# Two cross-attention layers on one core: the first layer's output projection with three of its products split once more, and the second layer's queries spread over earlier work

## The chip, the cores and the metric

The kernel runs on one core of a Trainium2 chip. The metric is the time of one execution in microseconds (us). TensorE (PE in the profile) multiplies, VectorE (DVE) adds, ScalarE (ACT) evaluates functions and copies, GpSimd (POOL) does some elementwise work and issues some transfers, SyncE (SP) issues the others. All data are 32-bit floats.

## The reference, cut to what matters

Two cross-attention layers follow each other; B=8 batches of 100 rows with 1024 features attend to 1444 context rows with 512 features.

```python
# layer 0
Q = query @ Wq + bq;  K = ctx @ Wk + bk;  V = ctx @ Wv + bv
weights = softmax(Q @ K.T / 32)            # over the 1444 context rows
x = query + (weights @ V) @ Wo + bo
# layer 1: Q and K likewise from x and ctx, but the softmax runs over the 100 rows
w = softmax((x @ Wq + bq) @ (ctx @ Wk + bk).T / 32, axis=rows)
y = w @ (ctx @ Wv + bv) + x
out = (y - mean) * rsqrt(var + 1e-6) * gamma + beta
```

## The kernel before

**Weights first.** The kernel multiplies weights with each other, so that keys and values are never formed. For layer 0 it makes `wqk0` = Wq Wk^T (1024 x 512) and `wvo` = Wv Wo (512 x 1024), for layer 1 `wqk1`. "Queries" are then x times wqk, 512 features long, and are multiplied with the context itself. The attended context (512 long, `A0T`) is projected with `wvo` onto the residual `xT`.

**Seven products instead of eight.** Large products are cut into 2x2 blocks and computed with seven block products and sums of blocks (the Strassen-Winograd scheme). `seven_products` (L202) does this for the projections. S and T are the sums of left and right blocks; the banks X, Y, Z, W are accumulators in PSUM. Some block products are cut once more in the same way by `inner_product` (L255), a generator with seven steps, each one smaller product into one bank and its addition to the result. It keeps its second and fourth sums in the place of its operands, and makes them after its first and second product.

**PSUM.** There are eight accumulator banks: six in the pool that `bank` (L68) takes from, two in that of `bank2` (L71). `bank2` serves the weighted rows (`weighted_rows`, L831) and the products named z and w.

**Layer 0 per batch.** `alternated(b)` (L1130) runs 48 steps; each is one small matmul of the weighted context rows of batch b (tile A, line L837) and one piece of the scores of batch b+2 (tile s, line L866). For batches 6 and 7 there are no scores left.

**The projection** (`project0`, L956) has two halves, j=0 and j=1, for features 0 to 511 and 512 to 1023 of `xT`. Each is a `seven_products` with 400-wide right operands; a block product is four matmuls of 128x128 by 128x400. The first two products of half j=0 are issued between batches 6 and 7, the other twelve after batch 7. All their results are added to `xT` on VectorE. The sums of weight blocks are made during batch 1 (`value_sums`).

**The second layer's queries** (`queries(1, ...)`, L616) come next. The steps are X = A11 B11; then Y = S1 T1; an inner product z; X with S2 T2; X with S3 T3 alternating with an inner product w; and, after the scores of batch 0 of layer 1, Y with S4 B22. Their block products are eight matmuls of 128x128 by 128x400, their inner steps two of 128x128 by 128x200. The banks of X and Y hold over nearly all of this. The sums S1, S2 lie in tiles of the tag `row`, S3 and S4 in the place of `wqk1`. `key_bias_sums` (L590) adds eight scaled copies of `xT` on VectorE (tile `kb`), and `key_biases` (L603) reduces them to one number per row and batch (tile `c`); both stand after the first five query steps, and the scores of batch 0 come after them.

**What sets the order.** TensorE executes in program order (`manual_schedule`). On the other engines a planner orders the instructions, by the order of the program and by when it takes operands to be ready; an instruction wrapped in `keep_in_program_order` is pinned behind the instruction that stands before it on its engine. The object `vector` does this to every VectorE instruction issued while `vector.in_order` is true. In `project0` nothing is pinned; in the second queries most is.

**Buffers.** `unit` (L74) gives one of ten rotating 6 KB-per-partition buffers. The context tiles cT and c are loaded into them through SP's queue, each load waiting for its buffer to come free; scratch and constants of later stages use the same ten. The tag `AT` (two buffers) holds the attended context, later T1 and T2 of the queries; the tag `gT` (three) holds the queries and the projection's sums.

Of the kernel before, what the change touches and what calls it, by code (L numbers as in the profile page):

```python
# [25 lines left out]
F32 = mybir.dt.float32  # L26
AF = mybir.ActivationFunctionType
ALU = mybir.AluOpType
# [3 lines left out]
P = 128  # L32
# [23 lines left out]
def two_layer_cross_attention(ctx: ExitStack, tc: tile.TileContext, a: dict, out: bass.AP):  # L56
# [11 lines left out]
    def bank(name):  # L68
        return psum.tile([P, 512], F32, tag="ps", name=name)

    def bank2(name):  # L71
        return psum2.tile([P, 512], F32, tag="ps2", name=name)

    def unit(name):  # L74
        return stream.tile([P, E + L], F32, tag="unit", name=name)

    def wide(name):
        return work.tile([P, LC, GT], F32, tag="AT", name=name, bufs=2)

    def row(name):  # L80
        return work.tile([P, E], F32, tag="row", name=name, bufs=3)
# [98 lines left out]
    def combine(to, x, y, op, engine=vector):  # L180
        for t, p, q in zip(to, x, y):
            engine.tensor_tensor(t, p, q, op)
# [69 lines left out]
        add(0, 1, Y)  # L252
        yield

    def inner_product(name, lhs, rhs, nb, width, t, put, add, right=None):  # L255

        h, w = nb // 2, width // 2

        def quarters(x, n):
            if len(x) == 1:
                return ([x[0][:, 2 * k : 2 * k + 2, c]] for c in halves(n) for k in range(2))
            return ([x[2 * k + i][:, c] for i in range(2)] for c in halves(n) for k in range(2))

        def room(x, t):
            t = t.rearrange("p (i n) -> p i n", i=2)
            return [t] if len(x) == 1 else [t[:, i, :] for i in range(2)]  # L270

        A11, A12, A21, A22 = quarters(lhs, nb * P)
        B11, B21, B12, B22 = quarters(rhs, width)
        S1, T1 = room(lhs, t[:, : 2 * h * P]), room(rhs, t[:, 2 * h * P : 2 * h * P + 2 * w])

        T2, T3, T4 = B11, B12, B21
        if right:
            T1, T2, T3, T4 = right
        combine(S1, A21, A22, ALU.add)
        combine(T1, B12, B11, ALU.subtract)  # L280
        combine(A21, A11, A21, ALU.subtract)
        combine(T3, B22, B12, ALU.subtract)

        def product(ps, left, right, fresh):
            half_product([ps], left, right, fresh, h, w)

        def steps():
            X = bank(f"{name}_x")
            product(X, A11, B11, True)
            put(0, 0, X)  # L290
            combine(T2, B22, T1, ALU.subtract)
            combine(A11, S1, A11, ALU.subtract)
            yield
            Z = bank2(f"{name}_z")
            product(Z, A12, B21, True)
            add(0, 0, Z)
            combine(T4, B21, T2, ALU.subtract)
            combine(A12, A12, A11, ALU.subtract)
            yield
            Y = bank(f"{name}_y")  # L300
            product(Y, S1, T1, True)
            put(1, 1, Y)
            yield
            product(X, A11, T2, False)
            put(0, 1, X)
            yield
            W = bank2(f"{name}_w")
            product(W, A22, T4, True)
            put(1, 0, W)
            yield  # L310
            product(Y, A12, B22, False)
            add(0, 1, Y)
            yield
            product(X, A21, T3, False)
            add(1, 1, X)
            add(1, 0, X)
            yield

        return steps()

    def halves(n):
        return slice(0, n // 2), slice(n // 2, n)
# [267 lines left out]
    def key_bias_sums(name, wqbk):  # L590

        acc = work.tile([P, B * T + P - T], F32, tag="kb", name=name, bufs=1)
        nc.gpsimd.memset(acc[:, B * T :], 0.0)
        for k in range(EC):
            if k == 0:
                nc.vector.tensor_scalar(acc[:, : B * T], xT[:, k, :], wqbk[:, k : k + 1], None, ALU.mult)
            else:
                nc.vector.scalar_tensor_tensor(
                    acc[:, : B * T], xT[:, k, :], wqbk[:, k : k + 1], acc[:, : B * T], ALU.mult, ALU.add
                )  # L600
        return acc

    def key_biases(name, kb, bqbk):  # L603

# [11 lines left out]
    def queries(layer, w, u, between=None):  # L616
# [4 lines left out]
        H, nb, h = EC // 2, 2, GT // 2  # L621
        A11, A12, A21, A22 = ([w[:, k * H : (k + 1) * H, j * 256 : j * 256 + 256]] for j in range(2) for k in range(2))
        B11, B21, B12, B22 = ([xT[:, k * H : (k + 1) * H, g * GT : g * GT + GT]] for g in range(2) for k in range(2))
        S1, S2 = ([row(f"g{layer}_s{n}").rearrange("p (c l) -> p c l", c=H)] for n in (1, 2))
        T1, T2 = ([wide(f"g{layer}_t{n}")] for n in (1, 2))
        T3 = [work.tile([P, LC, GT], F32, tag="gT", name=f"g{layer}_t3", bufs=3)]
        dst = [work.tile([P, LC, GT], F32, tag="gT", name=f"g{layer}T_{g}", bufs=3) for g in range(2)]

        def put(r, g, banks):
            for j in range(2):  # L630
# [20 lines left out]
            return put, add  # L651

        def pair(n):
            return [bank(f"g{layer}_{n}{j}") for j in range(2)]

        def product(banks, lhs, rhs, fresh):
            half_product(banks, lhs, rhs, fresh, nb, GT)

        t = unit(f"g{layer}_t")

        def inner(n, lhs, rhs, put, add, right=None, at=0):
            return inner_product(f"g{layer}_{n}", lhs, rhs, nb, GT, t[:, at:], put, add, right)

        def four(t):

            return [[t[:, n, :].rearrange("p (i t) -> p i t", i=2)] for n in range(4)]

        def steps():
            X = pair("x")
            product(X, A11, B11, True)  # L670
            put(0, 0, X)
            yield
            S3, S4 = A21, A12
            if layer == 0:
                Z = pair("z")
                product(Z, A12, B21, True)
            vector.in_order = layer == 0
            combine(S1, A21, A22, ALU.add)
            vector.in_order = True
            combine(T1, B12, B11, ALU.subtract)  # L680
            combine(S2, S1, A11, ALU.subtract)
            if layer == 0:
                combine(T2, B22, T1, ALU.subtract)
                vector.in_order = False
                yield
                vector.in_order = True
                add(0, 0, Z)
            combine(S3, A11, A21, ALU.subtract)
            if layer == 0:
                combine(T3, B22, B12, ALU.subtract)  # L690
            Y = pair("y")
            product(Y, S1, T1, True)
# [22 lines left out]
            V = half_steps(X, S3, T3, False, nb, GT)  # L715
            for n, _ in enumerate(inner("w", A22, T1, *parts(1, 0))):
                next(V)
                if layer == 0 and n == 1:
                    between()
                elif layer == 0 and n == 3:  # L720

                    add(0, 1, Y)
                    _, more = parts(0, 1)
                    Q = inner("q", S4, B22, more, more, four(T2[0]), 768)
# [62 lines left out]
    run(steps)  # L787
    wqbk0 = totals("wqbk0", sums_c, 2 * EC)
    nc.vector.tensor_tensor(out_bias, out_bias, wqbk0[:, EC:], ALU.add)
    kb0 = key_bias_sums("kb0", wqbk0[:, :EC])  # L790
    wqk1, (acc_c, acc_u) = next(qk1)
    c0 = next(got[0])
    for t in prob:
# [161 lines left out]

    def project0(AS, A0):  # L956

        Bs = [[A0[g][:, 2 * k + i, :] for i in range(2)] for g in range(2) for k in range(2)]
        t12, t4 = (work.tile([P, LC, GT], F32, tag="gT", name=f"o0_t{n}", bufs=3) for n in (12, 4))
        T_ = ([t12[:, i, :] for i in range(2)], [t12[:, 2 + i, :] for i in range(2)], Bs[2], chunks(t4, 2))  # L960
        for j, (A, S) in enumerate(AS):

            def add(r, g, banks, j=j):
                e = 4 * j + 2 * r
                add_to_queries([e, e + 1], g * GT, GT, banks)

            right = None if j else (lambda n: right_sums(Bs, T_, (n,)))
            yield seven_products(f"o0_{j}", A, Bs, S, T_, 2, GT, add, add, right=right)


    def softmax1(s, parts):
# [174 lines left out]
    first_transposed(batches[0], 0)  # L1146
    run(steps)
    for b in range(B):
        if b == B - 1:

            o0 = list(project0(AS, A0))
            next(o0[0])
            next(o0[0])
        run(alternated(b, 0, softmax0, A0[b // G][:, :, b % G * T : (b % G + 1) * T]))
        for e in range(2 * b, 2 * b + 2) if 2 * b < EC else ():
            add_out_bias(e)
        if b == 0:
            sums = quarter_sums("k1")
            block_sums("u1", acc_u, sums[:, :LC, :], late=True)
            block_sums("wqbk1", acc_c, sums[:, LC : LC + EC, :], late=True)  # L1160
        if b == 1:
            got = totals("k1", sums[:, : LC + EC, :], LC + EC)
            u1, wqbk1 = got[:, :LC], got[:, LC:]
            vector.in_order = True
            AS = value_sums(wvo)
            vector.in_order = False
    next(o0[1])
    for steps in o0:
        run(steps)

    gT[1], steps = queries(1, wqk1, u1)
    run(islice(steps, 5))
    kb1 = key_bias_sums("kb1", wqbk1)
    *_, key_bias[1] = key_biases("c1", kb1, bqbk1)
    vectors = [unit(f"vectors_{j}") for j in range(2)]
    gamma, beta = (t[:, :E] for t in vectors)
    bv1 = [t[:, E:] for t in vectors]
# [5 lines left out]
    nc.gpsimd.dma_start(out=wv1, in_=a["L1_xattn_Wv"].rearrange("(c p) e -> p c e", p=P))  # L1183


    run(first_scores(0, 1, softmax1))
    run(steps)
    run(first_scores(1, 1, softmax1))

# [44 lines left out]
```

## Time and profile before

| | |
|---|---|
| median of three runs | 635.28 us (633.83 to 636.32) |
| the profiled execution | 635.93 us, of which the span from first to last instruction is 634.0 us |
| granted TensorE clock | 0.997 of full speed |
| TensorE busy | 623.5 us of the span (98%) |
| VectorE busy | 480.7 us (76%) |
| ScalarE, GpSimd busy | 157.3 us (25%), 93.5 us (15%) |
| weighted rows of batch 6, two products, weighted rows of batch 7 | 321.9 to 349.6 us |
| the other twelve products of the projection | 349.6 to 381.8 us |
| second queries up to the first scores of layer 1 | 381.8 to 413.4 us |

A line of the timeline gives start, duration, engine, source line, operation, tiles (written<-read) with the shape, and how many instructions were merged; idle time before it and what ended that stand in brackets. One 32-bit matmul shows as two records. The ends of matmuls are modelled and overlap the next start by 0.16 to 0.17 us, so durations of TensorE are taken from start to start. L163 and L96 are lines of helpers, which is why the tile's name counts there. "PEld" is the load of the stationary operand, which overlaps.

### The profile page before, as it was taken

Reading aid. Unit: us, or ns where it says so; the run is one execution under the profiler, and the core shown is the slowest. Engines: PE = TensorE matmul, PEld = TensorE weight load, DVE = VectorE, ACT = ScalarE, POOL = GpSimd, SP = SyncE. Lnnn points to the kernel's source line nnn. Section 1 sums busy time; section 2 is a strip of 40 time slices with the busy share of each in tenths; the row PEclk is TensorE's granted clock in tenths of the full one; section 3 lists DMA queues with packets and bytes.
Section 4 is the critical chain, followed back from the end, with each engine's and each line's share of the span. In section 5 each row is a group of like instructions: output and inputs, shape, how many; then the busy total and the mean of one; then the engine's idle time right before and its main releaser. Section 6 shows DMA issues by size and latency. Waiting matters only on the chain.

```text
span 634.0 us, 10421 instructions
## 1 busy us (share of the span) xinstructions
PE 623.5 (98%) x4112; PEld 531.0 (84%) x4112; DVE 480.7 (76%) x948; ACT 157.3 (25%) x369; POOL 93.5 (15%) x123
## 2 busy tenths in 40 slices
PE   9999999999999999999999999999999999999994
PEld 8886466688985999999998556756999999999992
DVE  2987979998875797666753799549777659898886
ACT  1322010206204234423230001113433240325301
POOL 2110100002110000000000001008211220544054
PEclk9999999999999999999999999999999999999998
DMA  8969946015789899999965206155899890599002
GB/s 265 297 141 317 345 132 219 1 47 113 149 288 384 279 306 305 329 300 309 318 208 184 86 0 232 48 194 192 290 298 309 317 315 17 198 330 332 28 20 85
DMA packets 51077, 135.17 MB, mean 213 GB/s; under 512 B 4242, under 2 KB 8594, under 8 KB 51030
## 3 DMA queue, kind: packets, MB, share of 16 engines
q1 hardware_dynamic: 46792, 120.85, 55.7%
q0 software_dynamic: 3840, 13.20, 8.8%
q8 instruction: 32, 0.52, 0.3%
q10 hardware_dynamic: 398, 0.47, 0.2%
q14 instruction: 15, 0.12, 0.1%
HBM read 123.36 MB, written 3.28 MB: 200 GB/s over the span
## 4 chain that ended last, share of the span: by engine, by line
PE 94%; DVE 3%; issue 1%; POOL 1%; ACT 0%; POOLq 0%; DVEq 0%
PE s L866 25%; PE A L837 25%; PE qk_x L163 7%; PE o_x L163 5%; PE g_x L163 4%; PE vo_x L163 3%; PE o_y L163 3%; PE qk_z L163 2%; PE qk_y L163 2%; PE g_y L163 2%; PE o_w L163 2%; PE o_z L163 2%; PE qk_w L163 1%; PE vo_y L163 1%; PE vo_z L163 1%; PE z L1065 1%
## 5 line engine op out<-in xcount | busy, mean ns | idle before, releaser
L837 PE MATMUL A<-w,c 120*128 120x100 f32 (+1 forms) x1536 | 247.7, 265 | 0.0
L837 PEld LDWEIGHTS A<-w,c 120*128 120x128 f32 (+1 forms) x1536 | 215.9, 190 | 0.8
L96 DVE STREAM_TRANSPOSE w<-prob 32x384 f32<-32x384 f32 (+1 forms) x256 | 143.7, 561 | 35.1 <-ACT prob L878 15.7
L866 PE MATMUL s<-cT,g1T 128*100 128x131 f32 (+2 forms) x592 | 122.9, 296 | 0.3 <-DVE g1T L96 0.3
L866 PE MATMUL s<-cT,g0T 128*100 128x131 f32 (+2 forms) x592 | 122.7, 296 | 0.0
L866 PEld LDWEIGHTS s<-cT,g1T 128*100 128x100 f32 x592 | 78.3, 167 | 9.3 <-DVE g1T L96 1.2
L866 PEld LDWEIGHTS s<-cT,g0T 128*100 128x100 f32 x592 | 78.2, 167 | 8.4 <-PE c L566 0.4
L878 ACT ACTIVATE prob<-s,c 100x393 f32<-100x393 f32 (+2 forms) x64 | 35.1, 560 | 112.7 <-PE s L866 112.4
L988 ACT ACTIVATE w<-w,negmax 120x100 f32<-120x100 f32 (+1 forms) x96 | 34.8, 364 | 82.4 <-DVE negmax L96 82.4
L898 DVE TENSOR_REDUCE maxima<-prob 100x1 f32<-100x394 f32 (+3 forms) x32 | 16.5, 528 | 24.3 <-ACT prob L878 24.0
L163 PE MATMUL qk_x<-qk 128*128 128x256 f32 x128 | 30.5, 388 | 0.0
L1183 POOL DMA_DIRECT2D wv<-in_L_xattn_Wv x1 | 0.8, 772 | 200.1 <-PE o_x L163 200.1
L1007 POOL TENSOR_TENSOR part<-w 120x500 f32<-120x500 f32 x8 | 10.9, 1363 | 113.0 <-DVE rstd L1082 28.6
L163 PEld LDWEIGHTS qk_x<-qk 128*128 128x128 f32 x128 | 24.0, 196 | 3.2 <-ACT qk L413 0.2
L632 ACT ACTIVATE g1T<-g_x,k 128x400 f32<-128x400 f32 x4 | 2.4, 594 | 69.2 <-PE g_x L163 69.0
L533 POOL DMA_DIRECT2D qk_L_xattn_bk<-qk_L_xattn_bk x5 | 4.4, 937 | 102.6 <-ACT qk_L_xattn_bk L530 92.0
L96 DVE TENSOR_TENSOR xT<-xT,o_x 128x400 f32<-128x400 f32 (+1 forms) x32 | 15.8, 539 | 4.5 <-PE o_x L163 4.3
L988 ACT ACTIVATION_READ_ACCUMULATOR w<-w,negmax 120x1 f32 (+1 forms) x96 | 17.9, 187 | 0.0
L1087 POOL TENSOR_TENSOR z<-z,vectors 100x1024 f32<-100x1024 f32 x7 | 16.5, 2357 | 8.2 <-ACT z L1086 8.2
L1065 PE MATMUL z<-ident,xT 128*100 128x128 f32 x64 | 16.3, 273 | 0.0
L96 DVE TENSOR_TENSOR w<-w,rtotal 120x400 f32<-120x400 f32 (+1 forms) x24 | 15.6, 648 | 0.7
L1086 ACT ACTIVATE z<-z,rstd 100x1024 f32<-100x1024 f32 x7 | 8.1, 1150 | 31.9 <-POOL rstd L1083 31.9
(340 smaller groups left out, 961.5 us busy)
## 6 DMA issues: line engine op xcount, KB each, us to landing
cT<-in_ctxT SPq DMA_DIRECT2D x64, 722.0 KB, 6.5
c<-in_ctx SPq DMA_DIRECT2D x48, 768.0 KB, 7.9
c<-in_ctx SPq DMA_DIRECT2D x16, 512.0 KB, 7.3
vo<-in_L_xattn_Wo SPq DMA_DIRECT2D x8, 512.0 KB, 9.8
qk<-in_L_xattn_WqT SPq DMA_DIRECT2D x8, 512.0 KB
qk<-in_L_xattn_WqT SPq DMA_DIRECT2D x15, 256.0 KB, 6.2
c<-in_ctx SPq DMA_DIRECT2D x16, 224.0 KB, 6.2
xT<-in_xT SPq DMA_DIRECT2D x2, 1600.0 KB
```

The source lines that it names most:

```text
L96: ins = getattr(nc.vector, op)(*args, **kw)
L163: nc.tensor.matmul(banks[n // per][:, n % per * width : (n % per + 1) * width], lhs[i][:, n * P : (n + 1) * P], rhs[i], start=(fresh and i ...
L533: nc.gpsimd.dma_start(out=to, in_=t, accum_op=ALU.add)
L837: nc.tensor.matmul(ps[:, k * T : (k + 1) * T], c[m // CQ][:r, m % CQ, k * P : (k + 1) * P], w[:r, m, :], start=(m == 0 and k == 0), stop=( ...
L866: nc.tensor.matmul(banks[n // per][:T, cuts[n] - o : cuts[n + 1] - o], q[:, k, t0 : t0 + T], cT[k][:, cuts[n] : cuts[n + 1]], start=(k == ...
L878: nc.scalar.activation(p[:, part], ps[:T, : part.stop - part.start], AF.Identity, bias=key_bias[layer][:T, b : b + 1], scale=SCALE,)
L898: nc.vector.tensor_reduce(maxima[:, n : n + 1], p[:, part], AX.X, ALU.max)
L988: nc.scalar.activation(w[:r, m0 + m, :], w[:r, m0 + m, :], AF.Exp, bias=negmax[:r, m : m + 1], accum_out=total[:r, m : m + 1])
L1007: add(part, w[:MR, 0:5, :], w[:MR, 5:10, :], ALU.add)
L1065: nc.tensor.transpose(ps[:T, e * P : (e + 1) * P], xT[:, 4 * j + e, b * T : (b + 1) * T], ident)
L1086: nc.scalar.activation(z, z, AF.Copy, scale=rstd)
L1087: nc.gpsimd.tensor_tensor(z, z, beta[:T], ALU.add)
```

## The change

- `inner_product` works for operands of two pieces as well as four, and can make all its eight sums ahead of its products, into scratch (`ahead`). `spare` says which pool its banks z and w come from.
- `project0` is written out: both halves run interleaved in one order. Three products of half j=1 (z, w and q) are split by `inner_product`; the others stay. The first two products of half j=0 are issued one matmul at a time among the 48 steps of batch 6, and the seven steps of the split z among those of batch 7. From batch 7 on, VectorE's instructions are pinned.
- `queries(1)`: the sums S1, S2, S3 are issued during batch 7, T1 in the middle of the projection. S1 and S2 lie in `unit` buffers. The banks of Y come from the pool of two, those of the inner products all from the pool of six. In layer 0's queries the sum S1 is no longer pinned.
- The eight additions of `kb` for layer 1 are issued one by one from query step n=3 on; their reduction follows, pinned; its last part (one matmul and three small VectorE instructions) stands before the last two matmuls of the first scores.

```diff
-    def inner_product(name, lhs, rhs, nb, width, t, put, add, right=None):
+    def inner_product(name, lhs, rhs, nb, width, t, put, add, right=None, ahead=False, spare=bank2):
...
         combine(S1, A21, A22, ALU.add)
         combine(T1, B12, B11, ALU.subtract)
-        combine(A21, A11, A21, ALU.subtract)
+        combine(S3, A11, A21, ALU.subtract)
         combine(T3, B22, B12, ALU.subtract)
+        if ahead:
+            second()
+            fourth()
...
-            Z = bank2(f"{name}_z")
+            Z = spare(f"{name}_z")
             product(Z, A12, B21, True)
             add(0, 0, Z)
-            combine(T4, B21, T2, ALU.subtract)
-            combine(A12, A12, A11, ALU.subtract)
+            if not ahead:
+                fourth()
...
         def pair(n):
-            return [bank(f"g{layer}_{n}{j}") for j in range(2)]
+
+            return [(bank2 if layer and n == "y" else bank)(f"g{layer}_{n}{j}") for j in range(2)]
...
+            spare = bank if layer else bank2
+            return inner_product(f"g{layer}_{n}", lhs, rhs, nb, GT, t[:, at:], put, add, right, spare=spare)
...
+            if layer:
+                combine(S1, A21, A22, ALU.add)
+                yield
+                combine(S2, S1, A11, ALU.subtract)
+                yield
+                combine(S3, A11, A21, ALU.subtract)
+                yield
+            T1, T2 = ([wide(f"g{layer}_t{n}")] for n in (1, 2))
+            if layer:
+                combine(T1, B12, B11, ALU.subtract)
+                yield
...
             for n, _ in enumerate(inner("w", A22, T1, *parts(1, 0))):
                 next(V)
+                if layer:
+                    yield
...
+        yield first()
+        vector.in_order = True
+        yield inner("z", 1, 0, 0, A_[1], B21, room[:, :512], right)
+        combine(T1, B12, B11, ALU.subtract)
+        X_ = pair("x")
+        product(X_, A_[0], B11, True)
+        combine(T2, B22, T1, ALU.subtract)
+        add(1, 0, 0, X_)
+        Y = pair("y")
+        product(Y, S[0], T1, True)
+        combine(T4, B21, T2, ALU.subtract)
+        combine(T3, B22, T3, ALU.subtract)
+        add(0, 1, 1, Y)
+        product(X, S[1], T2, False)
+        add(0, 0, 1, X)
+        W = pair("w", bank2)
+        product(W, A[3], T4, True)
+        add(0, 1, 0, W)
+        W = inner("w", 1, 1, 0, A_[3], T4, room[:, 512:])
+        product(X, S[2], T3, False)
+        add(0, 1, 1, X)
+        add(0, 1, 0, X)
+        product(Y, S[3], B22, False)
+        add(0, 0, 1, Y)
+        yield
+
+        Y = pair("y")
+        product(Y, S_[0], T1, True)
+        Q = inner("q", 1, 0, 1, S_[3], B22, room[:, :512], right)
+        add(1, 1, 1, Y)
+        product(X_, S_[1], T2, False)
+
+        next(W)
+        add(1, 0, 1, X_)
+        run(W)
+        add(1, 0, 1, Y)
+        product(X_, S_[2], T3, False)
+        run(islice(Q, 4))
+        add(1, 1, 1, X_)
+        add(1, 1, 0, X_)
+        run(Q)
+        vector.in_order = False
...
+            more = next(o0)
+            if b == B - 1:
+                gT[1], queries1 = queries(1, wqk1, u1)
+            for n, _ in enumerate(steps):
+                if n % 4 == 3 and n > 4:
+                    next(more, None)
+                    if b == B - 1 and n < 16:
+                        next(queries1)
...
-    next(o0[1])
-    for steps in o0:
-        run(steps)
-
-    gT[1], steps = queries(1, wqk1, u1)
-    run(islice(steps, 5))
-    kb1 = key_bias_sums("kb1", wqbk1)
-    *_, key_bias[1] = key_biases("c1", kb1, bqbk1)
+    next(o0)
+    next(queries1)
+    run(o0)
+
+    kb1, more = key_bias_sums("kb1", wqbk1)
+    steps = queries1
+    for n, _ in enumerate(islice(steps, 5 + 7)):
+        if n > 2:
+            vector.in_order = True
+            next(more, None)
+    run(more)
+    biases1 = key_biases("c1", kb1, bqbk1)
+    next(biases1)
+    vector.in_order = False
...
-    run(first_scores(0, 1, softmax1))
+    scores1 = first_scores(0, 1, softmax1)
+    run(islice(scores1, LC * NB - 2))
+    key_bias[1] = next(biases1)
+    run(scores1)
     run(steps)
     run(first_scores(1, 1, softmax1))
```

`first` is the generator of the first two products (A[0] with B11, A[1] with B21), one matmul per step; `add(j, r, g, banks)` adds two banks to block row r and column half g of half j; `inner` wraps `inner_product` with an `add` of 200 columns per bank and `ahead=True`.

## The prediction

> **What bounds the kernel now.** I read the page first, then TensorE's waits, busy time by stage, and the timelines of the stretch that the change rewrites.
>
> ```profile
> PE 623.5 (98%) x4112; PEld 531.0 (84%) x4112; DVE 480.7 (76%) x948; ACT 157.3 (25%) x369; POOL 93.5 (15%) x123
> PE warm L108 <- DVE ones L105: 1.1, 1, 1.1
> PE vo_x L163 <- ACT vo L413: 0.7, 1, 0.7
> PE s L866 <- DVE g1T L96: 0.3, 1, 0.3
> 349.60:381.80 32.20, 32.20 (x98) 18.23 (x97) 26.87 (x44) 0.00 (x0) 2.18 (x4) 1.00 0.11 36
> 381.80:413.40 31.60, 31.50 (x124) 21.71 (x122) 24.53 (x41) 5.28 (x10) 0.71 (x2) 1.00 0.37 138
> 600.00:634.00 34.00, 25.71 (x193) 22.16 (x191) 26.34 (x48) 3.84 (x4) 16.73 (x14) 0.95 0.16 49
> ```
>
> TensorE is the bound. Of its 10.5 us of idle time 8.3 lie in the last 34 us, untouched here; in all of the projection and the second queries it names one wait of 0.3 us. Busy time hides small lateness, though, so I go by starts. TensorE, then VectorE:
>
> ```profile
> 379.15 2.85 PE L163 MATMUL o_y<-A0T,o_s 128*128 128x400 f32 x8
> 381.83 5.54 PE L163 MATMUL g_x<-xT,qk 128*128 128x400 f32 x16
> 387.21 5.54 PE L163 MATMUL g_y<-g_t,g_s 128*128 128x400 f32 x16
> 392.58 0.84 PE L163 MATMUL g_z_x<-xT,qk 128*128 128x200 f32 x4
> 397.08 0.84 PE L163 MATMUL g_z_x<-g_t,qk 128*128 128x200 f32 x4
> 397.76 5.54 PE L163 MATMUL g_x<-g_t,g_s 128*128 128x400 f32 x16
> 413.24 0.30 PE L566 MATMUL c<-c_sums,same 128*128 128x32 f32 x2
> 413.38 0.83 PE L866 MATMUL s<-cT,g1T 128*100 128x361 f32 x2
> 414.55 9.37 PE L866 MATMUL s<-cT,g1T 128*100 128x361 f32 x30 [0.34 <-DVE g1T L96]
> 383.54 3.23 DVE L598 SCALAR_TENSOR_TENSOR kb<-xT,k,kb 128x800 f32<-128x800 f32 x3
> 386.87 1.25 DVE L96 STREAM_TRANSPOSE c_t<-kb 128x1024 f32<-128x1024 f32 x1
> 397.29 0.36 DVE L96 TENSOR_TENSOR g1T<-g1T,g_z_y 128x200 f32<-128x200 f32 x1 [0.31 <-PE g_z_y L163]
> 397.96 0.63 DVE L96 TENSOR_TENSOR g1T<-g1T,g_z_x 128x200 f32<-128x200 f32 x2 [0.32 <-PE g_z_x L163]
> 347.08 3.01 SPq L805 DMA_DIRECT2D cT<-in_ctxT  x2
> 406.70 0.33 SPq L805 DMA_DIRECT2D cT<-in_ctxT  x1
> ```
>
> Prices from these. Four 400-wide matmuls take 381.83 - 379.15 = 2.68 us, 2.69 over the twelve products (32.26/12): 0.672 a matmul. A 200-wide one takes half, 0.336 (two in 397.76 - 397.08 = 0.68). The seven z steps take 397.76 - 392.58 = 5.18 where 14 x 0.336 = 4.70 are due: 0.48 late, behind VectorE's kb and c work. The second s matmul is due 0.60 after 413.38 (9.2/15 a matmul) and comes at 414.55: 0.56 late, for a bank that still held X.
>
> [...] The trace has 0.20 (the 128-wide vo_t sums, two before the next starts at 0.40) and 0.27 (start to start of paired 200-wide additions, from PSUM too[...]). [...]
>
> **The change, part by part.**
>
> *TensorE's work.* Before: 14 projection products x 2.69 = 37.66. After: 11 x 2.69 + 3 x 7 x 0.336 = 29.59 + 7.06 = 36.65. That is **-1.01**, and TensorE being the bound it counts in full where no wait eats it. Spreading the first products and z among the weighted rows changes no count. A row step costs 10.70/48 = 0.223 alone and about 0.21 beside scores (0.428 a pair, less 0.219 for 131 columns at 0.605 per 361), so a gain of up to 15 x 0.014 = 0.2, or as much loss; I take 0.
>
> *VectorE's work.* Each split adds four 128-wide and four 200-wide sums, 4 x 0.20 + 4 x 0.27 = 1.88, and makes eight additions of 0.27 out of two of 0.49 (400-wide, start to start): +1.18. Three splits: +9.2 us. z's sums are pinned behind the copy of batch 6's rows at about 339 and end near 341.4; its first sum is needed at step n=15 of batch 7, about 343. S1, S2, S3 (1.13 each) go under batch 7, where VectorE now idles 10.1 us. The rest fits: from batch 7's end to the first scores I count 54 us of VectorE work in 61 us.
>
> *The split w.* Here seven products follow each other every 0.336, while VectorE, pinned, must do W.x's addition, two 400-wide additions of X, then z, y, x ... Counting from W.x's start: it ends 0.34; addition from 0.55 (0.21 from a product's end to VectorE, as 397.08 to 397.29) to 0.82; X to 1.80; z to 2.07; y to 2.34, written 0.08 later. The sixth product reuses Y's bank and is due at 5 x 0.336 = 1.68; it can start at about 2.47: **+0.79**. The seventh then finds X free. In the split q four products stand before the large additions and the last three don't wait; z has four row steps between products. If only half of the lateness is real: +0.4; if each of the additions drags by 15%: +1.3.
>
> *The second queries.* kb (8 x 0.97) and c's transpose and reduction (2.3) leave the time ahead of z. S4 is pinned and overwrites an operand of g_x, so VectorE idles for about 3 us until g_x ends; its sums and T2 are then ready while g_y runs. The z steps keep about 0.18 of their 0.48: **-0.30** (0 to -0.48). Then VectorE runs without a gap: T3, T1, one kb, w's sums, and one kb after each w step. w's fifth product needs T4 with 1.3 us to spare. VectorE ends its additions about 2.9 us after TensorE's last V; before, it was 1.6.
>
> *The first scores.* That lateness costs nothing while the four banks of s don't hold X: z and w of the inner products now come from the six, so four others are free: **-0.50** of the 0.56. If the planner gives s an X bank instead, the wait returns as 1.0 to 2.0. Scores use the late block of g1T only at their ninth matmul, 4.8 us in. c's matmul merely moves (0.14 either way); its three small VectorE instructions, 0.6 us, end about when the last scores do. Behind them queue ScalarE's four evictions, then the transposes: batch 0's first rows are ready 1.4 us before TensorE reads them, which covers a c up to 1.4 late. Y's banks in the pool of two come free for batch 0's rows at 434.6 (first addition 434.04 + 0.57), 4 us before use.
>
> *Buffers and queues.* Three more `unit` buffers are taken ahead of batch 7's context and held to 381 to 402. That pushes the last of its loads from 318 to about 326, when batch 6's rows free buffers; they land in 7.3, so at 334, before use at 338.9 and later. Of the first two score batches' context, the last load waits for g_t as today (406.70, after 347.08), three others for o0_t, S1, S2; needed past 427. SP's queue therefore stays hidden. POOL's loads keep their trigger, the last read of wvo.
>
> *Layer 0's S1 unpinned.* 1.13 us of VectorE may float ahead of the pinned chain: 0, or up to +0.6 if it lands in front of vo's last sums; I take 0, as its consumer g_y starts 5 us after its inputs.
>
> **Sum.** -1.01 + 0.79 - 0.30 - 0.50 = **-1.0**. The profiled execution: 634.0 - 1.0 = 633.0 of span plus 1.9 around it = 634.9. It lay 0.65 above the median of the runs, so as a median 635.28 - 1.0 = **634.3 us**, 0.2% less: within 0.5% (3.2 us), about what a measurement of this kernel tells from no change.
>
> **Rivals.**
>
> 1. *All waits go.* No stall in w, all of 0.48 and 0.56 back, 0.2 from interleaving: -1.01 - 1.04 - 0.2 = -2.25, 633.0. For it: VectorE has 7 us of slack over the stretch. Against: w's additions stand locally behind the X pair.
> 2. *Savings given back.* w stalls 1.3, z stalls stay, s waits 1 us for an X bank: -1.01 + 1.3 + 0.5 = +0.8, 636.1. For it: the pinned order has no room to go around a late product. Same side of 0.5% as the forecast.
> 3. *Slower: VectorE becomes the bound.* From g_x's end it has some 30 us of gapless pinned work with about 50 instructions, and TensorE reads from it all along. If pinned, dependent instructions cost 0.09 us more each (15%), it ends 4.5 us later, and stalls in w, z and s reach 4 to 5: -1.0 + 4.5 = +3.5, 638.8. It decides from about +0.085 us each. Against: dependent additions in today's pinned stretches already run at the spacing used (kb at 0.97).
> 4. *The change does nothing*: counts are fixed by the program, so only waits could cancel it; that is rival 2.
>
> A gain over 3.2 us has no source: everything findable sums to 2.3.
>
> **Chances.** Forecast (633.3 to 635.2): 0.55. Rival 1: 0.12. Rival 2, up to 637: 0.20. Rival 3 and anything slower past 638.5: 0.10. More than 3.2 us faster: 0.03. Faster, same, slower by 0.5%: 0.03, 0.87, 0.10. The range, 632.4 to 637.0, takes in rivals 1 and 2 with half a us of measurement spread; the forecast's own is 633.3 to 635.2.
>
> **What would show it.** Right: 21 o records groups of 200 columns with starts 0.336 apart; a gap near 0.8 before w's sixth product, released by VectorE; z steps of g within 0.2 of 4.70; no wait at the first s; the stretch from batch 6's rows to the first s about 1 us shorter, everything after it shifted alike. Wrong: a TensorE wait over 1 us anywhere from 320 to 440; context loads landing after their use; s waiting for g1T; VectorE without idle time between 380 and 415; changed spacing in the rows of batches 6 and 7.

## The result and the profile after

The changed kernel takes 637.54 us (median of 5 runs, 636.80 to 638.99) where the kernel before takes 635.23 (5 runs beside it, 633.83 to 636.32): a ratio (changed over before) of 1.0039 with a 95% interval of 1.0027 to 1.0052. The prediction was 634.3 with a range up to 637.0, so the sign was wrong and the time lies above the range. The loss, 2.3 us, is still less than 0.5%.

The profiled execution of the changed kernel took 637.29 us, 635.2 of it span. Its page gives the engines' busy times:

```profile
PE 622.7 (98%) x4130; PEld 532.9 (84%) x4130; DVE 489.4 (77%) x992; ACT 156.7 (25%) x369; POOL 93.6 (15%) x123
```

TensorE is busy 0.8 us less than before and the span is 1.2 us longer. The answer must lie in the idle time, so TensorE's waits come next (total, times, longest in us):

```profile
PE vo_x L163 <- DVE vo_s L96: 1.5, 1, 1.5
PE warm L108 <- DVE ones L105: 1.1, 1, 1.1
PE vo_q_x L163 <- DVE vo L96: 0.9, 1, 0.9
PE o_w_y L163 <- DVE xT L96: 0.6, 1, 0.6
```

The third line is new, the first is twice what it was, and both belong to `vo`, the weight product Wv Wo that is made at 53 to 102 us (`vo_q_x`, `vo_w_x` and so on are steps of its block products q and w, which are split once more). The wait at the first s is gone. The wait in the split w (`o_w_y`) is the one that was forecast. Busy time by stage, of the rows of batches 6 and 7 with what is issued among them, the rest of the projection, and the queries up to the first scores (a line gives the stretch, its length, the busy time and count of PE, PEld, DVE, ACT and POOL, the granted clock, the busy share of the DMA engines and GB/s):

```profile
323.31:353.61 30.30, 30.30 (x234) 27.97 (x233) 21.19 (x45) 3.73 (x5) 0.00 (x0) 1.00 0.33 111
353.61:383.54 29.93, 29.37 (x103) 18.26 (x102) 24.62 (x60) 0.00 (x0) 1.99 (x4) 1.00 0.12 37
383.54:414.91 31.37, 31.37 (x122) 21.53 (x122) 25.82 (x47) 5.27 (x10) 0.92 (x2) 1.00 0.56 211
```

From the last s of layer 0 (323.31) to the last block product of the queries, g_y (424.84), the changed kernel takes 101.53 us; before, it was 423.75 - 321.66 = 102.09. **The stretch that the change rewrites is 0.56 us faster.** (Up to the first s alone it is 91.60 instead of 91.72; most of the gain comes with the scores.) The loss is elsewhere. TensorE's timeline of the changed kernel, of the stretch and of `vo`:

```profile
52.77 7.11 PE L163 MATMUL vo_x<-vo 128*128 128x512 f32 x16
75.14 7.11 PE L163 MATMUL vo_x<-vo,vo_s 128*128 128x512 f32 x16 [1.52 <-DVE vo_s L96]
96.72 1.03 PE L163 MATMUL vo_q_y<-vo_t 128*128 128x256 f32 x4
98.69 1.13 PE L163 MATMUL vo_q_x<-vo 128*128 128x256 f32 x4 [0.95 <-DVE vo L96]
99.66 1.09 PE L163 MATMUL vo_q_w<-vo 128*128 128x256 f32 x4
100.63 1.13 PE L163 MATMUL vo_q_y<-vo 128*128 128x256 f32 x4
102.46 0.29 PE L585 MATMUL u<-u_sums,same 128*128 128x16 f32 x2
...
375.13 0.50 PE L163 MATMUL o_w_x<-o_t,vo 128*128 128x200 f32 x2
376.53 0.50 PE L163 MATMUL o_w_w<-o_t,vo 128*128 128x200 f32 x2
377.59 0.60 PE L163 MATMUL o_w_y<-o_t,o_t 128*128 128x200 f32 x2 [0.56 <-DVE xT L96]
378.37 2.85 PE L163 MATMUL o_x<-A0T,vo 128*128 128x400 f32 x8
381.06 0.50 PE L163 MATMUL o_q_x<-A0T,o_s 128*128 128x200 f32 x2
383.54 1.84 PE L163 MATMUL g_x<-xT,qk 128*128 128x400 f32 x5
394.28 0.84 PE L163 MATMUL g_z_x<-xT,qk 128*128 128x200 f32 x4
399.42 5.54 PE L163 MATMUL g_x<-g_t,g_s 128*128 128x400 f32 x16
```

From the first vo_x to u, the small matmul that closes the stage, it takes 102.46 - 52.77 = 49.69 us. Before, the same two starts lay 47.47 apart (53.34 and 100.81): **+2.22**. VectorE's timeline of the changed kernel shows what is new in there:

```profile
67.75 0.74 DVE L96 TENSOR_SCALAR prob<-vo,L_xattn_bv 128x1024 f32<-128x1024 f32 x1
68.41 1.22 DVE L96 TENSOR_TENSOR g_s<-qk 128x1024 f32<-128x1024 f32 x1
69.55 3.92 DVE L96 SCALAR_TENSOR_TENSOR prob<-vo,L_xattn_bv,prob 128x1024 f32<-128x1024 f32 x3
...
91.04 0.70 DVE L577 STREAM_TRANSPOSE qk_L_xattn_bq<-qk_L_xattn_bq 128x512 f32<-128x512 f32 x1
91.67 1.78 DVE L96 TENSOR_TENSOR g_t<-xT 128x1600 f32<-128x1600 f32 x1
93.37 0.67 DVE L580 TENSOR_REDUCE u_sums<-qk_L_xattn_bq 128x16 f32<-128x512 f32 x1
```

Two instructions of layer 0's queries stand in the middle of `vo`: the sum S1 (g_s) at 68.41 and the sum T1 (g_t, 1600 columns) at 91.67. Before, VectorE did them when `vo` was over:

```profile
103.29 1.22 DVE L96 TENSOR_TENSOR g_s<-qk 128x1024 f32<-128x1024 f32 x1
104.42 1.82 DVE L96 TENSOR_TENSOR g_t<-xT 128x1600 f32<-128x1600 f32 x1
```

S1 is the instruction that the change no longer pins. T1 is pinned, but behind the instruction ahead of it, which is S1; with S1 free, nothing holds T1 behind `vo` either. S1 takes 1.14 us (68.41 to 69.55) of a chain at whose end vo_x waits for a sum; T1 takes 1.70 (91.67 to 93.37) ahead of the sums that vo_q_x needs, after which vo_q's steps come 0.97 instead of 0.86 apart.

In the profiled executions, +2.22 in `vo`, -0.56 in the stretch and +0.1 after it, with 0.57 less ahead of `vo`, make the span's +1.2. The 0.57 is taken for no effect of the change: both kernels have the same instructions up to there, and in the profiles of kernels for which that holds vo_x starts anywhere from 52.39 to 53.67.

### The profile page after: what moved, and what is told of

It reads as the page before. It is cut to its first block, busy times and chain, and to the rows that moved or that the text cites. A ratio compares the mean times of both kernels' runs of the same rounds, so it can differ in the third digit from the quotient of the medians.

```text
span 635.2 us, 10511 instructions
## 1 busy us (share of the span) xinstructions
PE 622.7 (98%) x4130; PEld 532.9 (84%) x4130; DVE 489.4 (77%) x992; ACT 156.7 (25%) x369; POOL 93.6 (15%) x123
## 4 chain that ended last, share of the span: by engine, by line
PE 94%; DVE 3%; issue 1%; POOL 1%; ACT 0%; POOLq 0%; DVEq 0%
PE s L906 25%; PE A L877 24%; PE qk_x L163 7%; PE g_x L163 5%; PE o_x L163 5%; PE o_y L163 3%; PE g_y L163 3%; PE vo_x L163 2%; PE qk_y L163 2%; PE qk_z L163 2%; DVE vo L96 1%; PE o_z L163 1%; PE o_w L163 1%; PE qk_w L163 1%; PE vo_z L163 1%; PE z L1171 1%
## 5 line engine op out<-in xcount | busy, mean ns | idle before, releaser
L1175 DVE SCALAR_TENSOR_TENSOR z<-vectors,r,z 100x512 f32<-100x512 f32 x16 | 11.8, 741 | 4.9 <-PE z L1171 4.8
```

What stands on the lines that cost most here:

```text
L1175: nc.vector.scalar_tensor_tensor(z[:, half], bv1[j][:T], s["r"], ps[:T, :], ALU.mult, ALU.add)
```

## The experiments

Two theories were set against each other first. **A:** the loss is that of layer 0's S1, and pinning it again gives it back. **B:** it comes from the rewritten stretch, its buffers or banks. The expectation on record has a third, C: the longer program costs time of its own, wherever. "The stretch" is from the last s of layer 0 to the last g_y, "the vo stage" from the first vo_x to u.

**S1 pinned again**, in the kernel after:

```diff
                 product(Z, A12, B21, True)
+                vector.in_order = True
                 combine(S1, A21, A22, ALU.add)
```

> The changed kernel with one line undone: layer 0's query sum S1 is pinned again. Theory A (the unpinned S1, and T1 that is pinned only behind it, float ahead of the value-times-output weight sums and stall TensorE there): both waits of the changed kernel's vo stage go (1.5 us at vo_x back to about 0.7, 0.9 at vo_q_x to 0), the time falls by 2.0 to 2.4 us to about 635.3, that is 0 to 0.6 us below the kernel before. Rival B (the loss sits in the rewritten projection and queries): still 1.5 to 2.5 us slower than before. Rival C (the longer program costs time of its own, wherever): still slower, with the same busy stretches.

**S1 unpinned**, in the kernel before:

```diff
-            vector.in_order = layer == 0
             combine(S1, A21, A22, ALU.add)
```

> The kernel before with that one line changed alone: S1 of layer 0's queries unpinned. Theory A: vo_x and vo_q_x wait as in the changed kernel, 1.7 to 2.3 us slower than before (637.0 to 637.5). Rival B and C: no difference, within 0.3 us.

| kernel | median us (before beside it) | ratio, 95% | vo stage | stretch |
|---|---|---|---|---|
| before | 635.23 | | 47.47 | 102.09 |
| after | 637.54 (635.23) | 1.0039, 1.0027 to 1.0052 | 49.69 | 101.53 |
| after, S1 pinned | 635.30 (635.32) | 0.9997, 0.9989 to 1.0005 | 47.13 | 101.53 |
| before, S1 unpinned | 637.89 (635.32) | 1.0036, 1.0023 to 1.0049 | 49.70 | 102.11 |

One line moves the difference both ways: the kernel after gets back 2.2 us with S1 pinned, and the kernel before loses 2.6 with S1 free (1.7 to 2.3 were expected). TensorE's waits of the kernel before with only S1 unpinned are those of the changed kernel in `vo`, next to the old wait at the first s:

```profile
PE vo_x L163 <- DVE vo_s L96: 1.5, 1, 1.5
PE vo_q_x L163 <- DVE vo L96: 1.0, 1, 1.0
PE s L865 <- DVE g1T L96: 0.3, 1, 0.3
```

TensorE's timeline of the kernel after with S1 pinned has no gap in front of vo_q_x:

```profile
74.55 7.11 PE L163 MATMUL vo_x<-vo,vo_s 128*128 128x512 f32 x16 [0.39 <-DVE vo_s L96]
96.12 1.03 PE L163 MATMUL vo_q_y<-vo_t 128*128 128x256 f32 x4
96.99 1.03 PE L163 MATMUL vo_q_x<-vo 128*128 128x256 f32 x4
100.44 0.29 PE L585 MATMUL u<-u_sums,same 128*128 128x16 f32 x2
```

Of the two instructions T1 can be priced from these lines: from vo_q_y to u it is 5.74 with T1 in front (96.72 to 102.46) and 4.32 without (96.12 to 100.44), so 1.42. The other two profiles with T1 free, of the kernel before with S1 unpinned and of the kernel after once more, have 5.75.

S1 can't be priced by subtracting the two waits of vo_x, 1.52 and 0.39, though their difference is about as long as S1. vo_x also waits for the loads of Wv and Wo that VectorE's sums need, and these land at another time in every profile: in two later kernels with S1 pinned vo_x waits 1.57 and 1.68. What can be compared is the time from the last sum that a load of Wv releases to vo_x, in profiles in which VectorE waits for no load after it. VectorE in the kernel after (its vo_x, at 75.14, is shown above), then VectorE and TensorE in the kernel with w and q whole (below), where S1 is pinned:

```profile
61.25 0.42 DVE L96 TENSOR_TENSOR vo_s<-vo,vo 128x256 f32<-128x256 f32 x1 [2.92 <-DMA vo<-in_L_xattn_WvT]
...
62.73 0.42 DVE L96 TENSOR_TENSOR vo_s<-vo,vo 128x256 f32<-128x256 f32 x1 [3.98 <-DMA vo<-in_L_xattn_WvT]
75.61 7.11 PE L163 MATMUL vo_x<-vo,vo_s 128*128 128x512 f32 x16 [1.57 <-DVE vo_s L96]
```

With S1 in between it is 75.14 - 61.25 = 13.89 us, without 75.61 - 62.73 = 12.88 (two other profiles with S1 pinned: 12.88 and 12.89). S1 costs 1.01, and both together 2.4. Theory A holds. B falls, and so does C as the cause of this loss: the kernel with S1 pinned has as many instructions as the kernel after.

**T1 held**: in the kernel after, T1 is pinned behind the instruction that stands ahead of S1, while S1, and S2 with it, still float. The kernel after ran again on the same chip.

```diff
+                vector.in_order = True
+                combine(T1, B12, B11, ALU.subtract)
+                vector.in_order = False
                 combine(S1, A21, A22, ALU.add)
             vector.in_order = True
             if layer == 0:
-                combine(T1, B12, B11, ALU.subtract)
                 combine(S2, S1, A11, ALU.subtract)
```

> The changed kernel with layer 0's T1 issued ahead of S1 and pinned, so that it stays behind the weight sums; S1 is left unpinned and floats as before, and S2 with it. If T1's 1.74 us in front of vo's last split product is what stalls vo_q_x: that wait (0.9 us) goes, vo_q takes 1.2 to 1.4 us less, and the time is 1.0 to 1.5 us below the changed kernel. If S1 alone is the cost: the time stays within 0.4 us of the changed kernel.

> The changed kernel itself, on the same chip as the run before it: 2.0 to 2.7 us slower than the kernel before, as measured at first, with both waits of the vo stage.

Measured: 636.85 with T1 held (ratio 1.0027, 1.0014 to 1.0039) and 638.36 for the kernel after (1.0053, 1.0038 to 1.0069), before being 635.19. (For the kernel after 2.0 to 2.7 us of loss were expected; here it is 3.2.) The wait of vo_q_x is gone and vo_q_y to u takes 4.31 again (98.89 to 103.20), as priced. S2, now free too, went ahead of vo's last additions and made a wait of 0.65 at g_x. So holding T1 gives back part and leaves S1's part, with S2's in it. By the traces the two kernels should differ by 1.43 - 0.65 = 0.8. How the timed 3.2 us divide is not sharp: the medians of the times differ by 1.5 between the two kernels, those of the spans (634.7 and 635.05) by only 0.4.

The profiled execution of this kernel shows one thing more. TensorE began `vo` early in it (at 52.39), VectorE's last sum of Wv came at 61.71, S1 stood in the chain behind it, so vo_x waited 2.38 us, and the matmuls after the wait were slow. Busy time by windows from the wait on (the third number from the end is the granted clock):

```profile
73.00:75.60 2.60, 0.23 (x1) 0.02 (x1) 2.60 (x5) 0.58 (x1) 0.86 (x1) 1.00 1.02 410
75.60:79.00 3.40, 3.39 (x5) 1.47 (x6) 3.40 (x9) 0.00 (x0) 0.00 (x0) 0.55 1.02 246
79.00:82.40 3.40, 3.40 (x9) 1.49 (x8) 2.03 (x8) 0.00 (x0) 0.00 (x0) 0.94 0.02 4
```

The vo_x behind the wait took 84.25 - 75.61 = 8.64 us instead of 6.94: a loss of 1.7 on top of the wait. Over the whole execution the granted clock was 0.994. Of the six executions of the kernel after in this comparison two show 0.993 and spans of 637.2 and 637.5, where the other four have 634.8 to 635.2. They left no profile, so that the same thing happened in them is not shown, but they are part of the 3.2.

**The banks alone**: the kernel before with the second queries' Y in the pool of two and its inner z and w in the pool of six.

```diff
-            return [bank(f"g{layer}_{n}{j}") for j in range(2)]
+            return [(bank2 if layer and n == "y" else bank)(f"g{layer}_{n}{j}") for j in range(2)]
...
-            Z = bank2(f"{name}_z")
+            Z = spare(f"{name}_z")
...
```

> The kernel before with the pools alone changed: Y of the second queries in the pool of two, the inner products' z and w from the six. If the wait at the first scores of layer 1 was for a bank that held X: that wait goes and the time falls by 0.4 to 0.6 us. If it was for the late block of the queries (g1T): the wait stays and nothing changes. If something else comes to need the pool of two while Y holds it: slower.

634.71 against 635.32 (ratio 0.9996, 0.9983 to 1.0010); the stretch takes 101.60, 0.49 less than before, and the wait at the first s is gone: its s matmuls run on from 413.37 without a gap. This is the "first scores" term, at its predicted size; the time resolves no such amount.

**The lateness of w spread.** In the kernel after with S1 pinned, X's additions come first, and the steps of w alternate with the four matmuls of the next product:

```diff
-        next(W)
         add(1, 0, 1, X_)
-        run(W)
+        V = half_steps(X_, S_[2], T3, False, 2, GT)
+        for n, _ in enumerate(W):
+            if n > 1:
+                next(V, None)
+        run(V)
         add(1, 0, 1, Y)
-        product(X_, S_[2], T3, False)
```

> S1 pinned, and the split product w issued between the four last matmuls of X instead of in a row, with X's additions ahead of w's. Theory (the row of seven products with 0.336 us between them outruns the pinned additions): its 0.89 us of lateness goes, 0.7 to 0.9 us faster than the kernel with S1 pinned alone, 1.2 to 1.5 below before. Rival (VectorE is the bound of the whole stretch, so the wait only moves on): the same time as with S1 pinned alone, with a new wait later.

635.61 against 635.32 (1.0001, 0.9993 to 1.0009), stretch 101.82, 0.29 longer than without. TensorE's timeline of this kernel says where it went: w and the product take 378.62 - 373.56 = 5.06 us, which is on time (2.35 + 2.69 = 5.04), but q now takes 3.64 instead of 2.47.

```profile
373.56 0.50 PE L163 MATMUL o_w_x<-o_t,vo 128*128 128x200 f32 x2
378.62 0.50 PE L163 MATMUL o_q_x<-A0T,o_s 128*128 128x200 f32 x2
380.74 0.60 PE L163 MATMUL o_q_x<-o_t,o_t 128*128 128x200 f32 x2 [0.57 <-DVE xT L96]
382.26 5.54 PE L163 MATMUL g_x<-xT,qk 128*128 128x400 f32 x16
```

The theory failed: VectorE's queue hadn't become shorter, and the stall only met the next product, as the rival had it. That VectorE is the bound of the whole stretch, the rival's reason, doesn't follow; the next experiment speaks against it.

**VectorE's queue shortened there.** The eight sums of q are made two products earlier, and X's additions stand ahead of w:

```diff
         add(0, 1, 1, Y)
+        Q = inner("q", 1, 0, 1, S_[3], B22, room[:, :512], right)
         product(X, S[1], T2, False)
...
-        Q = inner("q", 1, 0, 1, S_[3], B22, room[:, :512], right)
         add(1, 1, 1, Y)
         product(X_, S_[1], T2, False)
-        next(W)
         add(1, 0, 1, X_)
         run(W)
```

> S1 pinned; in the projection only VectorE's order changed: the split q's eight sums earlier (behind the first addition of Y), and X's two large additions ahead of w's first small one. Theory (w's seven products are late because the pinned order lets VectorE wait 0.4 us for w's first product and then puts 1 us of large additions before its small ones): w's start-to-start over seven products goes from 3.24 us to 2.35 to 2.5; 0.7 to 0.9 us of the trace's span below the kernel with S1 pinned alone. Rival (as when w was spread: the lateness moves to q): q's seven grow from 2.48 to 3.2 or more and the sum stays.

634.50 against 635.38 (0.9985, 0.9978 to 0.9991); the stretch takes 100.90. In TensorE's timeline w takes 2.62 us instead of 3.24 (2.35 to 2.5 were expected) and q stays at 2.47, so here the stall did not move on:

```profile
372.80 0.50 PE L163 MATMUL o_w_x<-o_t,vo 128*128 128x200 f32 x2
375.42 2.85 PE L163 MATMUL o_x<-A0T,vo 128*128 128x400 f32 x8
378.11 0.50 PE L163 MATMUL o_q_x<-A0T,o_s 128*128 128x200 f32 x2
380.58 5.54 PE L163 MATMUL g_x<-xT,qk 128*128 128x400 f32 x16
```

The two edits were not tried one by one.

**w and q whole again**, z still split, S1 pinned: both products are four 400-wide matmuls again, with two additions each.

```diff
-        W = inner("w", 1, 1, 0, A_[3], T4, room[:, 512:])
...
-        Q = inner("q", 1, 0, 1, S_[3], B22, room[:, :512], right)
...
+        W = pair("w", bank2)
+        product(W, A_[3], T4, True)
+        add(1, 1, 0, W)
...
+        product(Y, S_[3], B22, False)
+        add(1, 0, 1, Y)
```

> S1 pinned; w and q of the second half whole again, four 400-wide matmuls each; z stays split. TensorE's work grows by 2 x 0.336 = 0.67 us. If the two splits' waits (0.89 and 0.13 us) are their doing: 0.35 us faster than with S1 pinned alone. If the waits come from elsewhere and stay: 0.7 us slower.

634.24 against 635.38 (0.9985, 0.9978 to 0.9993). The products from 352.66 to 382.24 take 29.58 us, 0.35 less than the 29.93 of the split version. Two splits save 2 x 0.34 = 0.67 of TensorE's work and cost 0.89 + 0.13 = 1.02 in lateness; the difference is the 0.35.

```profile
352.66 2.88 PE L163 MATMUL o_x<-A0T,vo 128*128 128x400 f32 x8
382.24 5.54 PE L163 MATMUL g_x<-xT,qk 128*128 128x400 f32 x16
```

**The sums of the queries' z early.** T2 and T4 of layer 1's inner product z are made before its products instead of behind its first two additions:

```diff
         def second():
-            combine(T2, B22, T1, ALU.subtract)
+            if not early:
+                combine(T2, B22, T1, ALU.subtract)
...
+        if early:
+            combine(T2, B22, T1, ALU.subtract)
+            combine(T4, B21, T2, ALU.subtract)
```

> S1 pinned; in the second queries' split z the second and fourth right sums are made before its products, in VectorE's idle time under Y. Theory (z's lateness of 0.44 us is the two sums pinned behind the first and second additions): the seven steps take 4.70 to 4.80 us instead of 5.14, 0.4 us less. Rival (the prediction's: it came from the key-bias work ahead of z, which has moved): no change, since that work is no longer there.

634.85 against 635.38 (0.9992, 0.9983 to 1.0002). z takes 4.73 us (393.68 to 398.41) instead of 5.14; the time does not resolve these 0.4.

```profile
393.68 0.84 PE L163 MATMUL g_z_x<-xT,qk 128*128 128x200 f32 x4
398.41 5.54 PE L163 MATMUL g_x<-g_t,g_s 128*128 128x400 f32 x16
```

The cause is in VectorE's timeline of the kernel after:

```profile
395.23 0.36 DVE L96 TENSOR_TENSOR g1T<-g1T,g_z_x 128x200 f32<-128x200 f32 x1 [1.52 <-PE g_z_x L163]
395.51 0.57 DVE L96 TENSOR_TENSOR g_t<-xT,g_t 128x400 f32<-128x400 f32 x1
396.00 0.42 DVE L96 TENSOR_TENSOR qk<-g_t,qk 128x256 f32<-128x256 f32 x1
```

VectorE idles 1.52 us until z's first product is there, and only then makes T2 and S2; the fourth product reads both and starts at 396.47, 0.05 after S2 ends (396.00 + 0.42).

**Both together**: the shorter queue for w and q, and z's early sums, the last two edits on these sums in one kernel.

> All of it: S1 pinned, q's sums early, X's additions first, z's two sums early. The sum of the parts: 1.1 to 1.4 us below the kernel with S1 pinned alone, 1.6 to 2.0 us (0.25 to 0.31%) below the kernel before, whose median it then beats clear of the interval. If VectorE as a whole is the bound of the stretch: no more than 0.5 us below.

634.17 against 635.38 (0.9985, 0.9977 to 0.9992); stretch 100.50, the shortest, 1.59 less than before. Its z takes 396.19 - 391.45 = 4.74. So in the trace the parts add up (1.6 to 2.0 below the kernel before were expected), but the time falls by only 1.2: these executions have 2.2 us outside the span on average, where the kernel before has 1.9 (below).

Three versions (q's sums earlier, w and q whole, both together) beat the kernel before by about 0.15%, with intervals below 1. The times don't tell these three apart.

**Time outside the span.** The spans of the many runs gave a second, smaller part of the loss. In all 41 executions of kernels with w and q whole (before with S1 unpinned, before with new banks, after with w and q whole) 1.8 to 2.0 us of the time lie outside the span, as in every run of the kernel before beside them. In the kernels with w and q split, 30 of 104 executions have 2.4 to 3.7 outside, and the mean is 2.24 instead of 1.9. These kernels have 10510 or 10511 instructions, the others at most 10458. Two kernels tried whether the number does it: the kernel before with 96 tiny writes, once on GpSimd (the edit shown) and once on VectorE. They are issued along layer 0, but the planner moved them to the front (5.6 to 20.7 us and 1.0 to 47.6 us), so they test the number alone.

```diff
...
             next(ahead, None)
+            if layer == 0 and n % 4 == 0:
+                nc.gpsimd.memset(idle, 0.0)
             yield
```

> The kernel before with 96 more instructions, tiny writes of GpSimd to a tile that nobody reads, 12 in each batch of layer 0 (10517 instructions, as many as the kernel after has). Asked is the time outside the span alone: it was 1.8 to 2.0 us in every execution of kernels with up to 10458 instructions, and 2.4 to 3.7 in 30 of 104 of those with 10510 or 10511. If the mere number of instructions makes it, about 3 in 10 executions of this kernel have over 2.35 us outside the span, and the median rises by 0.1 to 0.4. If not, all stay at 1.8 to 2.0. The span itself should stay within 0.3 of the one before, as GpSimd has little to do in layer 0.

> The same with the 96 tiny writes on VectorE (1044 of its instructions instead of 948; the kernel after has 992, and the one with two whole products, which never showed it, 962). If VectorE's number of instructions makes the time outside the span longer, over 2.35 us shows here in about 3 in 10 executions and not in the GpSimd version; if the total number does, in both; if neither, in none. In the span, 96 x 0.06 us lie on VectorE beside work of TensorE and should show as 0 to 0.5 us.

All 26 executions stayed at 1.84 to 1.98 (medians 635.44 and 635.09, before 635.58). The number of instructions, in total or on these two engines, isn't the cause. That it comes with the splits of w and q is what the runs show: the kernel with w and q whole differs from the one with S1 pinned in this alone, and it has none in 22 where that one has 4 in 13. Why stays open.

## Why the prediction was wrong

**The step that failed is "Layer 0's S1 unpinned".** It was priced at 0, with +0.6 at most. It is worth +2.22 between the two traces of `vo`, 1.0 for S1 and 1.4 for T1 by the chains above, and 2.2 to 2.6 in the times with this one line changed. Three things were wrong with it. The slack looked at was that of S1's reader, g_y, which starts 5 us after its inputs; what counts is who stands behind S1 in VectorE's queue once it has moved, and that was vo_x, which in the trace before already waited 0.72 at that place (the trace names ScalarE, but vo_x starts 0.56 after VectorE's sums `vo_s` begin there, at 74.35; in the kernel after it is 75.14 - 74.58 = 0.56, with S1 pinned 74.55 - 73.98 = 0.57). It was looked at alone, although T1 is pinned to it and wider (1.70 against 1.14). And only one landing place, "in front of vo's last sums", was considered, where the planner found two.

**The rivals.** None was this one. Rival 3, the slower side, had VectorE become the bound in the stretch; it did not, since VectorE still idled there (3.07 us before S4 at 389.11) and no wait exceeded 0.6. Rival 2 gave +0.8 for a stretch that in fact gained.

**The sum of the stretch** was -1.0 and came to -0.56. By its terms:

- *TensorE's work*, -1.01: right. The 200-wide pieces start 0.34 apart (375.13 and 375.47 for the first two of w). The rows with matmuls issued among them cost +0.03 against 0.
- *VectorE's work*, +9.2: 489.4 - 480.7 = 8.7. Right.
- *The split w*, +0.79: w took 378.37 - 375.13 = 3.24 where 2.35 are due, +0.89. The mechanism was right: the sixth product waits 0.56 for VectorE, behind the two large additions; it starts at 377.59, 0.05 after the addition that reads its bank ends (377.19 + 0.35).
- *The split q*, 0: 383.54 - 381.06 = 2.48, +0.13.
- *The second queries' z*, -0.30: 399.42 - 394.28 = 5.14 after 5.18, so -0.04. The lateness was put down to kb and c work ahead of z. That work left, VectorE then idled 1.52 us, and z was as late as before, since its sums T2, S2, T4 and S4 are pinned behind its first additions. The version with early T2 and T4 takes 4.73. The work ahead of z can account for 0.11 at most: VectorE's first addition starts 0.95 after z does (394.28 to 395.23), and started 1.06 after it before (392.58 to 393.64). This term had the wrong cause.
- *The first scores*, -0.50: the s and c matmuls take 424.84 - 414.91 = 9.93 instead of 10.51, -0.58. Right.
- *Buffers and queues*, 0: right. No TensorE wait for a load appears in the stretch.

They add up to -1.01 + 0.03 + 0.89 + 0.13 - 0.04 - 0.58 = -0.58 (-0.56 between the starts).

**The total.** -0.56 + 2.22 + 0.1 = +1.8 for the span. The median of the spans over the eleven runs of the kernel after is 635.2; the kernel before has medians of 633.25 to 633.7 in the four comparisons: +1.5 to +1.95. The time outside the span is 0.35 us longer on average in the kernels with w and q split, and 0.7 in these eleven runs. Together that is 2.2 to 2.65, where 2.3 and 3.2 were timed: an account of the size, not a sharp one.

## What to carry to other kernels

An order constraint holds a chain by its first link: where a pin is taken from one instruction, everything that is pinned behind it can move too, and the price is found at the places where the chain can land, not at its reader. Ask of every freed instruction which pinned chain has a gap that it fits in, and who waits at that chain's end. A product that is split for less TensorE work paid here only where VectorE's extra sums and additions were out of the way before its products started; that decided between losing 0.35 us in the trace and gaining 0.28 (a stretch of 100.90 against 101.18 with w and q whole). In the times the gain does not show, 634.50 against 634.24, since the split version has the longer time outside the span.

## What was unexpected of the hardware

After a wait of 2.38 us, in the kernel with T1 held, TensorE's granted clock fell: 0.55 of full speed over the next 3.4 us (in other windows 0.50 from 76.0 to 78.0, 0.66 from 78.0 to 80.0 and 1.00 from 80.0 to 82.0), 1.7 us lost. It is one profile. Waits of 1.5 to 1.7 us at the same place (1.57 and 1.68 in two of the kernels) were followed by vo_x at its usual 6.94. The length of the wait alone doesn't decide it: at the end of the kernel before TensorE is idle from 625.7 us on, and the clock is still 1.00 in the window from 630.0 to 630.5, 0.87 in the next half us and 0.50 after it. What does decide it is not shown. In the profile in which it fell, a late sum in `vo` cost 1.7 us more than its lateness.

The last load of Wv that VectorE's sum vo_s needs let it go on at 59.58 to 62.73 us in profiles of kernels whose first 50 us are the same. Where it landed early, the sums after it waited for a load of Wo instead (1.67 us in the profile with 59.58). With that, and with where TensorE had got to, vo_x's wait moved between 0.4 and 1.7 us in the versions with S1 pinned. A wait of one profile is no price unless the loads are taken out of it.
